# Half-height sums joined by the vector engine and added to the image in the transfer, in place of unit-matrix products

## The chip, the cores and the metric

The kernel runs on one core of a Trainium2 chip. Its engines are PE (TensorE, matrix products; PEld is its loading of weights), DVE (VectorE), ACT (ScalarE), POOL (GpSimd) and SP (SyncE, which here only issues transfers). They run side by side and wait for one another by semaphores. Inputs and output lie in HBM; SBUF is the core's memory and PSUM the store into which PE writes. The metric is the device time of one execution in microseconds; lower is better.

## What is computed

160 images of 128 channels x 32 x 32 in float32. Each is group-normalised (32 groups of 4 channels), convolved 3 x 3 with the weights of its set (image index modulo 5 chooses one of 5 sets), and added to itself. The weights are quantised in two steps from U, with step sizes s1 and s2 that come from U's range:

```python
def _L0_conv_ref(x, U):
    s1 = (jnp.max(U) - jnp.min(U)) / 3.0
    v1 = s1 * floor(U / s1)
    s2 = s1 / 5.0
    v2 = s2 * floor((U - v1) / s2)
    w = (v1 + v2).reshape(OUT_CH * N, IN_CH, 3, 3)
    xb = x.reshape(B // 5, 5 * 128, 32, 32)
    return conv(xb, w, padding=1, feature_group_count=5)   # back to x's shape

def _gn(v, G=32, eps=1e-5):
    ...   # (g - mean) / sqrt(var + eps) over 4 channels x 32 x 32
x = x + _L0_conv_ref(_gn(x), L0_conv_U)
```

## The kernel before

The channels lie on the 128 partitions, and an image is 1024 float32 numbers on each. The 160 images are taken set by set, 32 of each; four images make a chunk (2 MB, tile `xt`), and six chunks have room in SBUF. The kernel writes its own order: nothing is scheduled for it, and each engine takes its instructions in the order in which `run` emits them. One pass of the loop in `run` is called iteration i below.

The weights are kept as small whole numbers (5 k1 + k2) in float16, so that w = s2 times them; what makes them, `make_column`, is spread over 26 iterations of the set before, two DVE steps in each, and ends with transposes on PE (`pt`), copies by ACT (`wt`) and sums by POOL.

For image i the steps are:

- `measure`: mean and variance of each channel, 13 images ahead. For even images DVE does it (`image`: BATCH_NORM_STATS2 on two halves and one aggregate, lines 156 and 157); for odd images, and the first eight, ACT does it in two passes (`image_sum` line 163, `image_square` line 172) that write a `junk` tile, and POOL scales the sums (`minus`, `mv`). The square needs `minus` from POOL.
- Once per group of images (2, 2, 4, 4, 4, then 8): `means`, `deviations`, `variances`, `scales` average over 4 channels with two small products on PE, and POOL makes `rstd` and `shift` (lines 202 to 207). `rstd` carries a factor of 512.
- `normalise` and `high_part`: ACT makes z = rstd x + shift in float32 (line 428) and `hi`, z in float16 (line 436), three images ahead.
- `low_part` and `combinations`: DVE makes `lo` = z - hi in float16 (line 441), its differences between rows two apart `d`, and sums and differences of pairs of rows `st` (lines 455 to 458), two images ahead.
- `conv`: PE makes from `st` two half-height products in the bank `m` (6 matrix products), and then in the bank `eo` the direct part, 9 taps on `hi` and corrections from `d` (30 matrix products). There is room for one `m` and two `eo`.
- `leave` (line 528): ACT copies `m` to SBUF as float16, scaled by 2^-10. `add_pairs` (lines 531 to 541): DVE adds and subtracts the two halves into `pq` (lines 537, 538), and PE adds `pq` to `eo` by two products with `up`, a unit matrix times 0.5 x 2^10.
- `residual` (line 550): DVE makes xt = s2z eo + xt in place, one iteration later, where s2z = s2 / 512. After the fourth image of a chunk SP stores the chunk (line 557). The last four images are stored one by one.

Images 0 to 2 are convolved directly from `hi` and `lo` (`conv_direct`), before there are weights and sums for the rest. A second, general path (`general_path`) stands behind a branch that is taken only if the flag `far`, worked out from U's range, is set; it isn't with these inputs.

Of the kernel before, what the change touches and what calls it, by code (L numbers as in the profile page):

```python
# [8 lines left out]
F32 = mybir.dt.float32  # L9
# [12 lines left out]
NB = 4  # L22
SCALE = 512.0
DOWN = 2.0**-10

# [5 lines left out]
class Steps:  # L31


    def __init__(self, nc, pool):
        self.nc = nc
        self.pool = pool
        self.s1, self.s2, self.s2z = (self.col(tag) for tag in ("s1", "s2", "s2z"))
# [9 lines left out]
    def from_range(self, extg):  # L47
# [27 lines left out]
        yield from parts(self.parts2, self.s2)  # L75
        yield nc.vector.tensor_scalar_mul(self.s2z, self.s2, 1.0 / SCALE)
# [57 lines left out]
class Statistics:  # L134

    def __init__(self, nc, small, psum, gavg, mhalf, nb, scale, name):
        self.nc, self.small, self.psum, self.gavg, self.mhalf = nc, small, psum, gavg, mhalf
        self.nb, self.scale, self.name = nb, scale, name  # L140
        self.mv = self.tile("mv", [nb, 2])
        self.minus = {}
# [55 lines left out]
    def scales(self):  # L198
        nc = self.nc
        ve = self.tile("ve", [self.nb])  # L200
        nc.scalar.copy(ve, self.pg[:, 1, :])
        nc.gpsimd.tensor_scalar(ve, ve, EPS, self.scale**-2, ALU.add, ALU.mult)
        self.rstd = self.tile("rstd", [self.nb])
        nc.gpsimd.tensor_tensor(self.rstd, ve, self.mhalf[:, : self.nb], ALU.pow)  # L204

        self.shift = self.tile("shift", [self.nb])
        nc.gpsimd.tensor_tensor(self.shift, self.ngm, self.rstd, ALU.mult)  # L207
# [68 lines left out]
class Main:  # L276
# [13 lines left out]


    STAT_LEAD = 13
    LOAD_LEAD = 17
# [7 lines left out]
    def __init__(self, tc, ctx, keep, x, u, out):  # L301
# [25 lines left out]
        self.steps = Steps(nc, keep)  # L327
        self.chunks, self.z, self.hi, self.v, self.eo, self.m = {}, {}, {}, {}, {}, {}
        self.wts = {}

# [50 lines left out]
    def make_column(self, n, col):  # L381
# [14 lines left out]
        wt = self.wpool.tile([P, 6, P], MM, tag=f"wt{col}", name=f"wt{n}_{col}")  # L396
        nc.scalar.copy(wt[:, self.G, :], pt)  # L397
        nc.scalar.mul(wt[:, self.MINUS_G2, :], pt[:, 2, :], -1.0)
        outer = self.qpool.tile([P, P], MM, tag="outer", name=f"outer{n}_{col}")
# [3 lines left out]
        self.wts[n, col] = wt  # L403


    def measure(self, i, stages=(0, 1)):


        k = self.group_of[i]
        g = self.groups[k]  # L410
        if k not in self.stats:
            self.stats[k] = Statistics(
                self.nc, self.small, self.ps_stat, self.gavg, self.mhalf, len(g), SCALE, k
            )
        st, j, image = self.stats[k], i - g.start, self.image(i)
        if i % 2 == 0 and i >= self.EARLY:
            st.image(j, image)
            return
        for s in stages:
            junk = self.evac.tile([self.P, 1024], MM, tag="junk", name=f"junk{i}_{s}")  # L420
            (st.image_sum, st.image_square)[s](j, image, junk)
# [72 lines left out]
    def conv(self, i):  # L494
# [22 lines left out]
        for col in self.COLS:  # L517
            self.taps(i, (self.hi[i], 0), col, eo, False)
            for a, kind in enumerate((0, self.MINUS_G2)):
                for h in range(2):  # L520
                    rows = slice(h * 16 + a, h * 16 + 16, 2)
                    to = eo[:, h].rearrange("p (i a) w -> p i a w", a=2)[:, :, a, :]
                    product(to, kind, d[:, rows, :], col, False, False)

    def leave(self, i):

        m = self.evac.tile([self.P, 2, 512], MM, tag="mm", name=f"mm{i}")
        self.nc.scalar.mul(m, self.m.pop(i).rearrange("p a i w -> p a (i w)"), DOWN)  # L528
        self.m[i] = m

    def add_pairs(self, i):

        nc = self.nc
        m = self.m.pop(i).rearrange("p a (i w) -> p a i w", w=self.W)
        pq = self.evac.tile([self.P, 2, 512], MM, tag="pq", name=f"pq{i}")
        rows = pq.rearrange("p h (i a w) -> p (h i) a w", a=2, w=self.W)
        nc.vector.tensor_add(rows[:, :, 0], m[:, 0], m[:, 1])  # L537
        nc.vector.tensor_sub(rows[:, :, 1], m[:, 0], m[:, 1])  # L538
        for h in range(2):
            to = self.eo[i][:, h].rearrange("p r w -> p (r w)")  # L540
            nc.tensor.matmul(to, self.up, pq[:, h], start=False, stop=True)  # L541

    def residual(self, i):
        eo = self.eo.pop(i)
        del self.hi[i]
        n, b = self.place(i)
        xj = self.image(i)
        halves = [slice(0, 512), slice(512, 1024)] if i == self.imgs - 1 else [slice(0, 1024)]
        for h in halves:
            self.nc.vector.scalar_tensor_tensor(  # L550
                xj[:, h], eo.rearrange("p h r w -> p (h r w)")[:, h], self.steps.s2z,
                xj[:, h], ALU.mult, ALU.add,
            )
            if i >= self.imgs - NB:
                self.nc.sync.dma_start(self.ov[n, :, b, h], xj[:, h])
        if i < self.imgs - NB and i % NB == NB - 1:
            self.nc.sync.dma_start(
                self.ov[n, :, b - NB + 1 : b + 1, :], self.chunks[i // NB]
            )

    def run(self):
# [17 lines left out]
        nc.gpsimd.tensor_copy(self.ident, ident)  # L579

        self.up = self.const.tile([P, P], MM, tag="up", name="up")
        nc.gpsimd.tensor_scalar_mul(self.up, ident, 0.5 / DOWN)
        self.gavg = group_mean_matrix(nc, self.const)
# [72 lines left out]
        self.conv_direct(2, 0)  # L656
        run(self.make_column(0, 2))
        ready, middle, measured, loaded, later = [], [], self.EARLY, 3, None
        for i in range(self.imgs):
# [16 lines left out]
            for k in to_measure:  # L676
                if k % 2:
                    self.measure(k, (0,))
# [11 lines left out]
            if i >= self.FIRST:  # L690
                self.add_pairs(i)
            for st in middle:
# [67 lines left out]
```

## Time and profile before

| | |
|---|---|
| median of 3 runs | 1168.15 us (1167.84 to 1168.36) |
| profiled execution | 1166.93 us, its span 1165.2 us |
| mean granted PE clock | 0.993 |
| busy, of the span | PE 96%, DVE 83%, ACT 59%, POOL 20% |
| DMA engines' share, in the steady state | 0.42, at 155 GB/s |
| HBM read and written | 86.84 MB and 83.89 MB |

The span runs from the first to the last instruction. A busy share says only how long an engine worked, not whether anybody waited for it; the chain of work that ended last says which engine's work set the end. A row of the lists by line gives the line, engine, operation, output from inputs, shape and count, then busy microseconds and mean nanoseconds of one, then the engine's idle time before them and what ended it. The first 75 us are a start in which weights, first statistics and first images are made one after the other; the steady state runs from there to about 1158 us.

### The profile page before, as it was taken

The numbers are of one execution on the slowest core, as the hardware profiler recorded it, in microseconds if no ns is written. First come the engines' busy times: TensorE is split into PE (matmuls) and PEld (weight loads), VectorE is DVE, ScalarE is ACT, GpSimd is POOL, SyncE is SP. The second block draws the span as 40 slices with busy tenths as digits, with TensorE's granted clock in tenths as the row PEclk, the third lists the DMA queues.
The fourth block names the chain that finished last, engine by engine and source line by source line (L and its number), as shares of the span: only waits on it lengthen the run. The fifth ranks groups of instructions, "written<-read, shape, count | busy, mean of one in ns | idle before, by whom it ended". The sixth has DMA issues, their size and how long they took to land.

```text
span 1165.2 us, 15925 instructions
## 1 busy us (share of the span) xinstructions
PE 1116.1 (96%) x6215; PEld 610.4 (52%) x6215; DVE 962.5 (83%) x1626; ACT 690.4 (59%) x891; POOL 234.5 (20%) x450
## 2 busy tenths in 40 slices
PE   0679999999999999999999999999999999999997
PEld 0335555555555555555555555555555555555554
DVE  7878988887798989878888887798989877777662
ACT  4666666656666566655665666656656666655441
POOL 3413312121113121202122221123122202021100
PEclk9889999999999999999999999999999999999999
DMA  9204444444333333333344444444333333331222
GB/s 363 99 39 151 162 156 165 161 171 156 145 145 145 145 145 145 145 145 145 145 162 166 162 161 179 167 154 154 145 145 145 145 145 145 145 145 73 87 96 109
DMA packets 43427, 171.82 MB, mean 147 GB/s; under 512 B 1488, under 2 KB 1488, under 8 KB 43344
## 3 DMA queue, kind: packets, MB, share of 16 engines
q1 hardware_dynamic: 43344, 170.73, 39.1%
q8 instruction: 50, 0.82, 0.3%
q14 instruction: 33, 0.27, 0.1%
HBM read 86.84 MB, written 83.89 MB: 147 GB/s over the span
## 4 chain that ended last, share of the span: by engine, by line
PE 95%; DVE 3%; ACT 1%; DMA 1%; POOL 0%; issue 0%; SPq 0%; DVEq 0%
PE eo L475 52%; PE eo L502 18%; PE m L502 18%; PE eo L541 6%; PE m L475 1%; DMA u<-in_L_conv_U_dram 1%; DVE ext L361 0%; DVE ext L362 0%; DVE xt L550 0%; DVE lo L441 0%; PE pg L196 0%; PE pg L181 0%; POOL rstd L204 0%; PE pt L395 0%; ACT z L428 0%
## 5 line engine op out<-in xcount | busy, mean ns | idle before, releaser
L475 PE MATMUL eo<-hi,wt 128*128 128x512 f16 (+1 forms) x2862 | 685.5, 376 | 1.1 <-ACT wt L397 1.1
L475 PEld LDWEIGHTS <-wt 128*128 128x128 f16 x2934 | 288.0, 98 | 276.2 <-issue 5.0
L502 PEld LDWEIGHTS <-wt 128*128 128x128 f16 x2826 | 276.7, 99 | 219.0 <-issue 4.4
L528 ACT ACTIVATE mm<-m 128x1024 f16<-128x1024 f32 x157 | 160.5, 1022 | 366.8 <-PE m L502 355.1
L502 PE MATMUL eo<-d,wt 128*128 128x256 f16 (+1 forms) x1884 | 283.2, 273 | 0.0
L550 DVE SCALAR_TENSOR_TENSOR xt<-eo,s2z,xt 128x1024 f32<-128x1024 f32 (+1 forms) x160 | 203.5, 1273 | 47.9 <-PE eo L541 40.1
L502 PE MATMUL m<-st,wt 128*128 128x512 f16 x942 | 230.4, 381 | 3.2 <-DVE xt L550 3.2
L428 ACT ACTIVATE z<-xt,shift,rstd 128x1024 f32<-128x1024 f32 x160 | 198.0, 1237 | 31.1 <-POOL shift L207 31.1
L441 DVE TENSOR_TENSOR lo<-z,hi 128x1024 f16<-128x1024 f32 x160 | 194.1, 1214 | 5.3 <-ACT hi L436 5.2
L537 DVE TENSOR_TENSOR pq<-mm 128x512 f16<-128x512 f16 x157 | 66.4, 423 | 122.9 <-ACT mm L528 122.7
L436 ACT CAST hi<-z 128x1024 f16<-128x1024 f32 x160 | 166.1, 1038 | 0.2
L165 POOL TENSOR_SCALAR minus<-total 128x1 f32<-128x1 f32 x84 | 47.3, 563 | 340.9 <-ACT junk L163 340.7
L455 DVE TENSOR_TENSOR d<-lo 128x1024 f16<-128x1024 f16 x157 | 109.5, 697 | 5.4
L172 ACT ACTIVATE junk<-xt,minus 128x1024 f16<-128x1024 f32 x84 | 96.7, 1152 | 1.0 <-POOL minus L165 1.0
L156 DVE BATCH_NORM_STATS2 st<-xt 128x6 f32<-128x512 f32 x152 | 97.2, 681 | 0.0
L163 ACT ACTIVATE junk<-xt 128x1024 f16<-128x1024 f32 x84 | 88.0, 1048 | 11.8 <-DMA xt<-in_x_dram 11.7
L175 POOL TENSOR_SCALAR mv<-squares 128x1 f32<-128x1 f32 x84 | 45.7, 545 | 237.5 <-ACT junk L172 234.9
L541 PE MATMUL eo<-pq,up 128*128 128x512 f16 x314 | 93.5, 380 | 0.0
L538 DVE TENSOR_TENSOR pq<-mm 128x512 f16<-128x512 f16 x157 | 65.6, 418 | 0.0
L457 DVE TENSOR_TENSOR st<-lo 128x512 f16<-128x512 f16 x157 | 65.6, 418 | 0.0
L458 DVE TENSOR_TENSOR st<-lo 128x512 f16<-128x512 f16 x157 | 65.4, 416 | 0.0
L204 POOL TENSOR_TENSOR rstd<-ve,mhalf 128x8 f32<-128x8 f32 (+2 forms) x23 | 43.9, 1907 | 1.9
(87 smaller groups left out, 421.1 us busy)
## 6 DMA issues: line engine op xcount, KB each, us to landing
xt<-in_x_dram SPq DMA_DIRECT2D x39, 2048.0 KB, 13.0
out_dram<-xt SPq DMA_DIRECT2D x39, 2048.0 KB, 7.6
u<-in_L_conv_U_dram SPq DMA_DIRECT2D x4, 576.0 KB, 8.1
xt<-in_x_dram SPq DMA_DIRECT2D x4, 512.0 KB, 10.7
out_dram<-xt SPq DMA_DIRECT2D x3, 512.0 KB, 2.7
u<-in_L_conv_U_dram SPq DMA_DIRECT2D x2, 288.0 KB, 3.0
out_dram<-xt SPq DMA_DIRECT2D x2, 256.0 KB, 3.5
```

The lines of the kernel that those rows point to most:

```text
L156: self.nc.vector.bn_stats(st[:, h, :], image[:, h * half : (h + 1) * half])
L163: nc.scalar.activation(junk, image, ACTF.Copy, accum_out=total)
L172: nc.scalar.activation(junk, image, ACTF.Square, bias=self.minus[j], accum_out=squares)
L428: nc.scalar.activation(z, self.image(i), ACTF.Identity, bias=st.shift[:, j : j + 1], scale=st.rstd[:, j : j + 1],)
L436: self.nc.scalar.copy(hi.rearrange("p h w -> p (h w)"), self.z[i])
L441: self.nc.vector.tensor_sub(lo[:, 1 : self.H + 1, :].rearrange("p h w -> p (h w)"), self.z.pop(i), self.hi[i].rearrange("p h w -> p (h w)"),)
L455: nc.vector.tensor_sub(d, lo[:, 0:H, :], lo[:, 2 : H + 2, :])
L475: nc.tensor.matmul(target[:, h, r0 - h0 : r1 - h0, c0:c1], self.wts[n, col][:, k, :], tile[:, s0 : s0 + r1 - r0, c0 + dw : c1 + dw], start ...
L502: nc.tensor.matmul(target[:, :, c0:c1], self.wts[n, col][:, kind, :], source[:, :, c0 + dw : c1 + dw], start=start, stop=stop,)
L528: self.nc.scalar.mul(m, self.m.pop(i).rearrange("p a i w -> p a (i w)"), DOWN)
L541: nc.tensor.matmul(to, self.up, pq[:, h], start=False, stop=True)
L550: self.nc.vector.scalar_tensor_tensor(xj[:, h], eo.rearrange("p h r w -> p (h r w)")[:, h], self.steps.s2z, xj[:, h], ALU.mult, ALU.add,)
```

## The change

- `add_pairs` becomes `pairs`: DVE makes `pq` as before, but PE no longer adds it. `up` and its two products per image are gone, and `eo` is finished by its last correction from `d`.
- `residual` makes, one iteration later, sum = 0.5/32 pq + eo into a tile `sum` (three of them). `accumulate` then adds `sum` to the image in its chunk by a transfer from SBUF to SBUF with an addition, issued from POOL's queue at the end of iteration i + 1. The chunk's store moves to the end of iteration i + 2 and waits for its four additions.
- Images 0 to 2 and the last four (`by_hand`) are added by DVE itself; for the last four that is one more operation in `pairs`.
- The step size moves into the images: `rstd` is multiplied by 2^14 s2 (through `shrink` = (1/s2 / 2^14)^2, made by DVE in the start, and used by POOL's line 217 in each group's `scales`), and the weights by 2^-14. `s2z` is gone. `far` now also looks at the size of s2, and is worked out in `choose`, after the columns of the first set.
- DVE does the statistics of one image in four (8, 12, 16, ...) instead of one in two; ACT does the others. `junk` gets a pool of its own with one buffer.

```diff
-        yield nc.vector.tensor_scalar_mul(self.s2z, self.s2, 1.0 / SCALE)
-        big, far = col("big"), col("far")
-        yield nc.vector.tensor_reduce(big, extg, AX.X, ALU.max)
-        yield nc.vector.scalar_tensor_tensor(far, span, WIDEST, big, ALU.mult, ALU.is_lt)
-        yield nc.vector.tensor_copy(self.far, far)
+        r = self.parts2[0]
+        yield nc.vector.scalar_tensor_tensor(self.shrink, r, LIFT**-2, r, ALU.mult, ALU.mult)
+        self.span, self.big = span, col("big")
+        yield nc.vector.tensor_reduce(self.big, extg, AX.X, ALU.max)
...
-        nc.gpsimd.tensor_scalar(ve, ve, EPS, self.scale**-2, ALU.add, ALU.mult)
+        nc.gpsimd.tensor_scalar(ve, ve, EPS, self.shrink, ALU.add, ALU.mult)
...
+        self.sums = pool("sums", 3)
+        self.unread = pool("unread", 1)
...
-        nc.scalar.copy(wt[:, self.G, :], pt)
-        nc.scalar.mul(wt[:, self.MINUS_G2, :], pt[:, 2, :], -1.0)
+        nc.scalar.mul(wt[:, self.G, :], pt, 1.0 / LIFT)
+        nc.scalar.mul(wt[:, self.MINUS_G2, :], pt[:, 2, :], -1.0 / LIFT)
...
+    def by_vector(self, i):
+        return i % 4 == 0 and i >= self.EARLY
...
-        if i % 2 == 0 and i >= self.EARLY:
+        if self.by_vector(i):
...
-        for h in range(2):
-            to = self.eo[i][:, h].rearrange("p r w -> p (r w)")
-            nc.tensor.matmul(to, self.up, pq[:, h], start=False, stop=True)
+        self.m[i] = pq
+        if self.by_hand(i):
+            xj = self.image(i)
+            nc.vector.scalar_tensor_tensor(xj, pq, 0.5 / UP, xj, ALU.mult, ALU.add)
+
+    def by_hand(self, i):
+        return i < self.FIRST or i >= self.imgs - NB

     def residual(self, i):
...
+        if not self.by_hand(i):
+            self.sum[i] = self.sums.tile([self.P, 1024], F32, tag="sum", name=f"sum{i}")
+            nc.vector.scalar_tensor_tensor(
+                self.sum[i], self.m.pop(i), 0.5 / UP, eo, ALU.mult, ALU.add
+            )
+            return
...
-            self.nc.vector.scalar_tensor_tensor(
-                xj[:, h], eo.rearrange("p h r w -> p (h r w)")[:, h], self.steps.s2z,
-                xj[:, h], ALU.mult, ALU.add,
-            )
+            nc.vector.tensor_add(xj[:, h], eo[:, h], xj[:, h])
...
+    def accumulate(self, i):
+        if i in self.sum:
+            self.nc.gpsimd.dma_start(self.image(i), self.sum.pop(i), accum_op=ALU.add)
+
+    def store(self, i):
+        if 0 <= i < self.imgs - NB and i % NB == NB - 1:
...
+            self.accumulate(i - 1)
+            self.store(i - 2)
             while loaded * NB < min(self.imgs, i + self.LOAD_LEAD):
                 self.load(loaded)
```

On PE, where one image ends and the next begins, the order before is this (`up` is the unit matrix, `m` and `eo` the banks, `d` and `st` the combinations of `lo`):

```order
L502 MATMUL eo_4911<-d_4829,wt_2_4771 128x8x31
L541 LDWEIGHTS up
L541 MATMUL eo_4911<-pq_4962,up 128x512
L541 LDWEIGHTS up
L541 MATMUL eo_4911<-pq_4962,up 128x512
L502 LDWEIGHTS wt_1_3585
L502 MATMUL m_4973<-st_4890,wt_1_3585 128x512
```

And this is the same place now:

```order
L526 LDWEIGHTS wt_2_4875
L526 MATMUL eo_5288<-d_5196,wt_2_4875 128x8x31
L526 LDWEIGHTS wt_2_4875
L526 MATMUL eo_5288<-d_5196,wt_2_4875 128x8x31
L526 LDWEIGHTS wt_1_3659
L526 MATMUL m_5365<-st_5259,wt_1_3659 128x512
```

The next image's first half product follows the last correction directly; nothing on PE reads `pq`.

On SP, in the middle of the program, stores and loads of chunks alternated like this before (the first number in a name is the chunk's):

```order
L557 DMA out_0_dram<-xt13_3039 128x4x1024
L346 DMA xt18_4424<-in_x_dram 128x4x1024
L557 DMA out_0_dram<-xt14_3302 128x4x1024
L346 DMA xt19_4704<-in_x_dram 128x4x1024
L557 DMA out_0_dram<-xt15_3600 128x4x1024
```

And now like this:

```order
L599 DMA out_0_dram<-xt12_2815 128x4x1024
L366 DMA xt18_4517<-in_x_dram 128x4x1024
L599 DMA out_0_dram<-xt13_3102 128x4x1024
L366 DMA xt19_4803<-in_x_dram 128x4x1024
L599 DMA out_0_dram<-xt14_3371 128x4x1024
```

The store of a chunk now stands one load later: the load of chunk 18 followed the store of chunk 13, and now follows that of chunk 12, whose room it takes.

On POOL, the statistics of consecutive images read now as follows (there was no transfer on this queue before):

```order
L594 DMA xt_1969<-sum_3229 128x1024
L594 DMA xt_1969<-sum_3291 128x1024
L180 TENSOR_SCALAR minus_3346<-total_3344 128x1
L181 TENSOR_SCALAR mv_3013<-total_3344 128x1
L190 TENSOR_SCALAR mv_3013<-squares_3365 128x1
L594 DMA xt_1969<-sum_3359 128x1024
L180 TENSOR_SCALAR minus_3416<-total_3414 128x1
```

An addition stands between one image's last statistic and the next one's first.

More of the change, by code (lines that the diff above doesn't have):

```diff
@@ L22 @@
 NB = 4
-SCALE = 512.0
-DOWN = 2.0**-10
+LIFT = 2.0**14
+LEAST, MOST = 2.0**-10, 0.06
+UP = 32.0
 WIDEST = 40.0
@@ L36, in __init__ @@
         self.pool = pool
-        self.s1, self.s2, self.s2z = (self.col(tag) for tag in ("s1", "s2", "s2z"))
+        self.s1, self.s2, self.shrink = (self.col(tag) for tag in ("s1", "s2", "shrink"))
         self.parts1, self.parts2 = (
@@ L75, in from_range, with choose @@
         yield from parts(self.parts2, self.s2)
-        yield nc.vector.tensor_scalar_mul(self.s2z, self.s2, 1.0 / SCALE)
-        big, far = col("big"), col("far")
-        yield nc.vector.tensor_reduce(big, extg, AX.X, ALU.max)
-        yield nc.vector.scalar_tensor_tensor(far, span, WIDEST, big, ALU.mult, ALU.is_lt)
-        yield nc.vector.tensor_copy(self.far, far)
+        r = self.parts2[0]
+        yield nc.vector.scalar_tensor_tensor(
+            self.shrink, r, LIFT**-2, r, ALU.mult, ALU.mult
+        )
+        self.span, self.big = span, col("big")
+        yield nc.vector.tensor_reduce(self.big, extg, AX.X, ALU.max)
+    def choose(self):
+        nc, far = self.nc, self.col("far")
+        nc.vector.scalar_tensor_tensor(
+            far, self.span, WIDEST, self.big, ALU.mult, ALU.is_lt
+        )
+        for limit, op in ((MOST, ALU.is_gt), (LEAST, ALU.is_lt)):
+            nc.vector.scalar_tensor_tensor(far, self.s2, limit, far, op, ALU.max)
+        nc.vector.tensor_copy(self.far, far)
     def floor_div(self, k, v, n, t, parts):
@@ L134, with __init__ @@
 class Statistics:
-    def __init__(self, nc, small, psum, gavg, mhalf, nb, scale, name):
+    def __init__(self, nc, small, psum, gavg, mhalf, nb, shrink, name):
         self.nc, self.small, self.psum, self.gavg, self.mhalf = nc, small, psum, gavg, mhalf
-        self.nb, self.scale, self.name = nb, scale, name
+        self.nb, self.shrink, self.name = nb, shrink, name
         self.mv = self.tile("mv", [nb, 2])
@@ L328, in __init__ @@
         self.chunks, self.z, self.hi, self.v, self.eo, self.m = {}, {}, {}, {}, {}, {}
+        self.sum = {}
         self.wts = {}
@@ L412, in measure @@
             self.stats[k] = Statistics(
-                self.nc, self.small, self.ps_stat, self.gavg, self.mhalf, len(g), SCALE, k
+                self.nc, self.small, self.ps_stat, self.gavg, self.mhalf, len(g),
+                self.steps.shrink, k,
             )
         st, j, image = self.stats[k], i - g.start, self.image(i)
-        if i % 2 == 0 and i >= self.EARLY:
+        if self.by_vector(i):
             st.image(j, image)
@@ L419, in measure @@
         for s in stages:
-            junk = self.evac.tile([self.P, 1024], MM, tag="junk", name=f"junk{i}_{s}")
+            junk = self.unread.tile([self.P, 1024], MM, tag="junk", name=f"junk{i}_{s}")
             (st.image_sum, st.image_square)[s](j, image, junk)
@@ L676, in run @@
             for k in to_measure:
-                if k % 2:
+                if not self.by_vector(k):
                     self.measure(k, (0,))
@@ L690, in run @@
             if i >= self.FIRST:
-                self.add_pairs(i)
+                self.pairs(i)
             for st in middle:
```

22 lines of the change are left out of this document (12 added, 10 removed).

## The prediction

> **What bounds the kernel now.** I read the page's busy line and its chain first, then the order of time on PE in the steady state, then the groups by line, then the other engines' load in one window.
>
> ```profile
> PE 1116.1 (96%) x6215; PEld 610.4 (52%) x6215; DVE 962.5 (83%) x1626; ACT 690.4 (59%) x891; POOL 234.5 (20%) x450
> PE 95%; DVE 3%; ACT 1%; DMA 1%; POOL 0%; issue 0%; SPq 0%; DVEq 0%
> L541 PE MATMUL eo<-pq,up 128*128 128x512 f16 x314 | 93.5, 380 | 0.0
> L528 ACT ACTIVATE mm<-m 128x1024 f16<-128x1024 f32 x157 | 160.5, 1022 | 366.8 <-PE m L502 355.1
> ```
>
> PE is busy for 96% of the span and makes 95% of the chain: from the first product on, the other engines only matter if they make PE wait. L528 waits 355.1 us for PE: ACT is ahead of it. The products to be removed are the 314 of L541. Their 380 ns each overlaps the next product, so the price is read from start to start (columns: start, duration, engine, line):
>
> ```profile
> 502.99 0.60 PE L541 MATMUL eo<-pq,up 128*128 128x512 f16 x2
> 503.42 1.46 PE L502 MATMUL m<-st,wt 128*128 128x512 f16 x6
> 509.84 0.60 PE L541 MATMUL eo<-pq,up 128*128 128x512 f16 x2
> 510.27 1.46 PE L502 MATMUL m<-st,wt 128*128 128x512 f16 x6
> ```
>
> A pair holds PE for 503.42 - 502.99 = 0.43 us, and an image takes 509.84 - 502.99 = 6.85 us.
>
> **Term 1, the products.** 157 images x 0.43 us = 67.5 us less on PE, all of it on the chain. An image then takes 6.42 us. Whether this is gained depends on what must now fit into 6.42 us.
>
> **DVE.** The columns are the window and its length, then busy time of PE, PEld, DVE, ACT and POOL, the granted clock, the DMA engines' share and GB/s.
>
> ```profile
> 300.00:600.00 300.00, 300.00 (x1689) 165.05 (x1687) 260.91 (x443) 185.24 (x237) 63.65 (x114) 1.00 0.42 155
> L550 DVE SCALAR_TENSOR_TENSOR xt<-eo,s2z,xt 128x1024 f32<-128x1024 f32 (+1 forms) x160 | 203.5, 1273 | 47.9 <-PE eo L541 40.1
> L156 DVE BATCH_NORM_STATS2 st<-xt 128x6 f32<-128x512 f32 x152 | 97.2, 681 | 0.0
> L157 DVE BATCH_NORM_AGGREGATE mv<-st 128x2 f32<-128x12 f32 x76 | 15.9, 209 | 4.0
> ```
>
> 300 us hold 300 / 6.85 = 43.8 images, so DVE works 260.91 / 43.8 = 5.96 us an image. The residual becomes an operation of the same size with one operand in PSUM and one in SBUF, as L550 has; I take its 1.27 us unchanged. The bounds are L550's own 1.27 us from below and, from above, 0.2 us more: such a slip would still fit. One image in four no longer has the statistics on DVE: (2 x 0.681 + 0.209) / 4 = 0.39 us less an image. That leaves 5.57 of 6.42 us, 87%, the share it has now. DVE's cover is thin but no thinner than before, and PE no longer waits for `pq` at all: the pair sums now feed the vector engine alone. What is queued behind DVE's wait for `eo` is as before. The four images added by hand at the end cost an extra 1.27 us each on DVE, where the last weights are long done; I count nothing, the cover being PE's 6.42 us an image.
>
> **ACT.** These rows are one image's ACT work with a statistics pass in it.
>
> ```profile
> 649.20 1.24 ACT L428 ACTIVATE z<-xt,shift,rstd 128x1024 f32<-128x1024 f32 x1
> 650.34 1.05 ACT L163 ACTIVATE junk<-xt 128x1024 f16<-128x1024 f32 x1
> ...
> 651.37 1.02 ACT L528 ACTIVATE mm<-m 128x1024 f16<-128x1024 f32 x1
> 652.28 1.05 ACT L436 CAST hi<-z 128x1024 f16<-128x1024 f32 x1
> 653.21 1.16 ACT L172 ACTIVATE junk<-xt,minus 128x1024 f16<-128x1024 f32 x1
> ...
> 654.36 1.24 ACT L428 ACTIVATE z<-xt,shift,rstd 128x1024 f32<-128x1024 f32 x1
> ```
>
> From z to z are 654.36 - 649.20 = 5.16 us. This is now wanted for three images of four instead of two. The pass is 651.37 - 650.34 = 1.03 plus 654.36 - 653.21 = 1.15, so the mean rises from 185.24 / 43.8 = 4.23 to 4.23 + 2.18 / 4 = 4.78 us of 6.42. Even the full image leaves 1.26 us. In iteration 8 the statistics of images 17, 18 and 19 come at once: two more passes make ACT up to 4.4 us late; the `m` bank is wanted back only when the next image begins, 6.42 less the 1.3 us of its products less 1.02 us of L528, about 4 us after ACT could first read it. I count nothing, with 1 us as the upper bound.
>
> **The transfers.** 153 images are added by a transfer from SBUF to SBUF issued on POOL's queue.
>
> ```profile
> q1 hardware_dynamic: 43344, 170.73, 39.1%
> xt<-in_x_dram SPq DMA_DIRECT2D x39, 2048.0 KB, 13.0
> out_dram<-xt SPq DMA_DIRECT2D x39, 2048.0 KB, 7.6
> xt<-in_x_dram SPq DMA_DIRECT2D x4, 512.0 KB, 10.7
> out_dram<-xt SPq DMA_DIRECT2D x3, 512.0 KB, 2.7
> ```
>
> The share of 0.42 is 0.42 x 6.85 = 2.88 us of all 16 engines an image, for 512 KB in and 512 KB out: 1.44 us for each. No row shows an adding transfer. From below it is a plain copy, 1.44 us; from above, unknown, call it f x 1.44. At f = 2, which I take because it moves one operand more than a copy, 5.76 of 6.42 us are used, 0.90, and nothing waits. DMA becomes the bound at f = (6.42 - 2.88) / 1.44 = 2.5 and eats the whole gain at (6.85 - 2.88) / 1.44 = 2.8.
> The Trainium skill's page "Collectives: The Full Stack", section "The bandwidth ceiling: the fold count and why AG ≠ RS ≠ AR", says that an addition in a DMA engine is slow only because it reads two sources, 1.93 times the cost of a copy there; by it f is about 2 and the sum stays. No run here shows it yet.
>
> Latency: an addition leaves at the latest one iteration after its sum and the three `sum` tiles give it two more, 12.8 us, against a landing of 2.7 us (a 512 KB store) to 10.7 us (a queued 512 KB load). SP's queue: the store now waits for the four additions, and the load behind it goes into the tile that is being stored, where before it went into one stored a chunk earlier. From the start of iteration 4c+5 the longest rows give 10.7 + 13.0 + 13.0 = 36.7 us, 5.7 images, so the load lands by 4c+10.7; its first reader is the statistic of image 4c+24 in iteration 4c+11. From below it is 2.7 + 7.6 + 7.6 = 17.9 us. Zero either way.
>
> **POOL.** It gets 153 issues, each behind a wait for DVE's sum; queued behind it are the next image's `minus` (for which ACT's square waits) and, eight images apart, `ve`, `rstd`, `shift`. In the rows above a square ends at 654.4 and the next one starts at 653.21 + 6.42 = 659.6; issue and `minus` must fit between, so an issue of up to 5 us costs nothing. No row shows one; the nearest, other POOL operations of 0.21 to 1.75 us (below), fit.
>
> **Term 2, the start.** `ve` of the first group now needs `shrink`, which DVE makes after the parts of s2, about where it made `s2z`.
>
> ```profile
> 26.04 0.36 POOL L202 TENSOR_SCALAR ve<-ve 128x2 f32<-128x2 f32 x1
> 27.48 0.14 DVE L76 TENSOR_SCALAR s2z<-s 128x1 f32<-128x1 f32 x1
> 37.65 1.23 DVE L441 TENSOR_TENSOR lo<-z,hi 128x1024 f16<-128x1024 f32 x1
> 68.37 1.28 DVE L156 BATCH_NORM_STATS2 st<-xt 128x6 f32<-128x512 f32 x2
> 69.68 0.21 DVE L157 BATCH_NORM_AGGREGATE mv<-st 128x2 f32<-128x12 f32 x1
> 69.81 1.17 DVE L441 TENSOR_TENSOR lo<-z,hi 128x1024 f16<-128x1024 f32 x1
> 73.62 2.72 PE m L502 x6
> ```
>
> `ve` moves from 26.04 to about 27.6, +1.6 us, and the first images behind it (the `lo` at 37.65 waits for them). Against it, image 10 leaves DVE, 69.81 - 68.37 = 1.4 us on the way to the first half product at 73.62; though ACT now does that pass, 2.18 us, and could give back 0.8 of it. Three tiny operations leave the chain (`far` comes back later, while DVE idles) and `shrink` joins it: 0.3 us less. Sum about 0, bounds -1.7 and +2.4.
>
> **Sum.** The profiled execution took 1166.93 us (span 1165.2 and 1.7 around it); 1166.9 - 67.5 = 1099.4. The median of the runs is 1.2 us above it, so 1100.6.
>
> **Rivals.**
> *A, the additions fill the DMA engines (slower).* For it: 0.42 is already used and an adding transfer reads more than it copies. Against: f must pass 2.8. At f = 3 an image takes 2.88 + 4.32 = 7.2 us, 157 x 0.35 = +55: 1223 us.
> *B, POOL's issues hold up DVE (slower).* These are POOL beside DVE:
>
> ```profile
> 307.28 1.75 POOL L204 TENSOR_TENSOR rstd<-ve,mhalf 128x8 f32<-128x8 f32 x1
> 307.42 1.22 DVE L441 TENSOR_TENSOR lo<-z,hi 128x1024 f16<-128x1024 f32 x1
> 316.30 1.17 POOL L166 TENSOR_SCALAR mv<-total 128x1 f32<-128x1 f32 x1
> 316.19 1.22 DVE L441 TENSOR_TENSOR lo<-z,hi 128x1024 f16<-128x1024 f32 x1
> 18.72 0.21 POOL L175 TENSOR_SCALAR mv<-squares 128x1 f32<-128x1 f32 x1 [0.92 <-ACT junk L172]
> ```
>
> A one-element POOL operation takes 0.21 us alone and 1.17 us under a DVE subtraction, ending with it: POOL is held by DVE. The other way is not seen: `lo` began 0.14 us into `rstd` and still took 1.22 us. If an issue did hold DVE for the longest of these, 1.75 us, DVE would need 5.57 + 1.75 = 7.32 us in the 128 images of the sets with weights in the making: +0.47 x 128 = +60, less 0.43 x 29 = 12: 1216 us. It decides from an issue of 6.85 - 5.57 = 1.28 us.
> The Trainium skill's page "SBUF — State Buffer", section "Who interferes with whom", states the lock for both sides: whoever starts first has the shared ports for the whole instruction. By it rival B would be likely; the row at 307.42 disagrees with it, that at 316.30 agrees.
> *C, part of the gain is lost at group and column starts.* z waits there for POOL's chain, and ACT's copies of weights wait for PE:
>
> ```profile
> ACT z L428 <- POOL shift L207: 31.1, 17, 3.8
> ACT wt L397 <- PE pt L395: 45.3, 15, 3.8
> ```
>
> If PE lost 0.6 us at each of these 32 places, 19 us would come back: 1120 us. Against it: L528's wait of 355.1 us, which is ACT's lead.
>
> **Chances.** Forecast 0.72, holding 1095 to 1106 (1100.6 with -1.7 to +2.4 of the start, 1 of ACT and the spread of runs, and small slips). C 0.10 (1106 to 1130). A 0.12: of it 0.02 lies between f of 2.5 and 2.8, still faster, and 0.10 is slower; B 0.04 slower; 0.02 that gains and losses cancel. A measurement of this kernel tells 0.2% (2.3 us) from no change. Faster 0.84, within 0.2% 0.02, slower 0.14. The range 1095 to 1127 leaves out A and B, a little of C and the low tail.
>
> **What would show it.** Right: PE's chain share still above 90%, image to image 6.42 us, no L541-like group, DVE near 87% and ACT near 75% in the steady window, DMA share near 0.9, and no row of PE waiting for ACT or DVE after 80 us. Term 2: POOL's first `ve` at about 27.6. Wrong: a DMA share of 1.0 with SP or DVE waiting for `sum` tiles (A); `lo`, `d` or `pq` longer than 1.22, 0.7 and 0.42 us beside POOL's issues (B); PE idle before `m` on ACT (C).

## The result and the profile after

The changed kernel takes 1100.56 us, the median of 4 runs (1100.23 to 1101.58), against 1168.07 us (1167.84 to 1168.36) for the kernel before: ratio 0.9423, 95% interval 0.9407 to 0.944. The forecast was 1100.6. The profiled execution took 1101.58 us, its span 1099.8 us.

The page of the changed kernel: busy time by engine, the new DMA queue (packets, MB, share of 16 engines' span), the chain by engine, the two largest new groups, and two kinds of DMA issue (count, KB each, us from issue to landing).

```profile
PE 1051.8 (96%) x5901; PEld 577.6 (53%) x5901; DVE 903.9 (82%) x1518; ACT 772.9 (70%) x1043; POOL 389.4 (35%) x716
...
q0 software_dynamic: 22032, 80.23, 38.9%
...
PE 94%; DVE 3%; DMA 1%; POOL 0%; ACT 0%; issue 0%; SPq 0%; DVEq 0%
...
L581 DVE SCALAR_TENSOR_TENSOR sum<-pq,eo 128x1024 f32<-128x1024 f16 x153 | 185.9, 1215 | 16.0 <-PE eo L526 15.8
...
L594 POOL DMA_DIRECT2D xt<-sum x153 | 136.6, 894 | 85.4 <-DVE sum L581 69.5
...
xt<-in_x_dram SPq DMA_DIRECT2D x39, 2048.0 KB, 13.5
...
xt<-sum POOLq DMA_DIRECT2D x153, 512.0 KB, 8.0
```

PE has 314 instructions fewer (5901 for 6215) and still makes 94% of the chain. The work that it lost rides along in DVE's residual, which is now the sum (L581, no longer than L550 was); adding to the image went to a new queue, q0, issued by POOL (L594), which takes 38.9% of what the 16 DMA engines have. The loads beside it land in 13.5 us where they took 13.0.

The steady window, with the columns of the one shown before, and then, from the order of time on PE, the starts of two images:

```profile
300.00:600.00 300.00, 300.00 (x1708) 165.89 (x1706) 259.16 (x440) 223.01 (x299) 114.44 (x195) 1.00 0.88 244
```

```profile
504.34 1.46 PE L526 MATMUL m<-st,wt 128*128 128x512 f16 x6
...
510.76 1.46 PE L526 MATMUL m<-st,wt 128*128 128x512 f16 x6
```

PE is busy for all of the 300 us at full clock. An image takes 510.76 - 504.34 = 6.42 us instead of 6.85. DVE stands at 259.16 / 300 = 86%, ACT at 74%, the DMA engines at 0.88 instead of 0.42.

The start, on PE, after and before: the first half product of image 3, and that of image 4.

```profile
74.07 2.72 PE L526 MATMUL m<-st,wt 128*128 128x512 f16 x6 [1.94 <-DVE xt L588]
...
83.55 1.46 PE L526 MATMUL m<-st,wt 128*128 128x512 f16 x6
```

```profile
73.62 2.72 PE L502 MATMUL m<-st,wt 128*128 128x512 f16 x6 [3.18 <-DVE xt L550]
...
82.28 1.46 PE L502 MATMUL m<-st,wt 128*128 128x512 f16 x6
```

Image 3 starts 0.45 us later than before. Its own length, to the start of image 4, is 9.48 us after and 8.66 us before, where 6.56 and 6.99 would be normal (6.42 and 6.85, with 0.14 for a small product in between). So image 3 loses 2.92 us to a slow clock, against 1.67 before: 1.25 more. Together the start costs +1.7 us in these two executions.

### The profile page after: what moved, and what is told of

Its sections match the earlier page's. It is cut to its first block, busy times and chain, and to the rows that moved or that the text cites. A ratio compares the mean times of both kernels' runs of the same rounds, so it can differ in the third digit from the quotient of the medians.

```text
span 1099.8 us, 16007 instructions
## 1 busy us (share of the span) xinstructions
PE 1051.8 (96%) x5901; PEld 577.6 (53%) x5901; DVE 903.9 (82%) x1518; ACT 772.9 (70%) x1043; POOL 389.4 (35%) x716
## 3 DMA queue, kind: packets, MB, share of 16 engines
q0 software_dynamic: 22032, 80.23, 38.9%
## 4 chain that ended last, share of the span: by engine, by line
PE 94%; DVE 3%; DMA 1%; POOL 0%; ACT 0%; issue 0%; SPq 0%; DVEq 0%
PE eo L499 55%; PE eo L526 19%; PE m L526 19%; PE m L499 1%; DMA u<-in_L_conv_U_dram 1%; DVE ext L381 0%; DVE ext L382 0%; DVE xt L588 0%; DVE lo L465 0%; PE pg L211 0%; PE pt L415 0%; ACT z L452 0%; PE pg L196 0%; ACT hi L460 0%; POOL rstd L219 0%
## 5 line engine op out<-in xcount | busy, mean ns | idle before, releaser
L465 DVE TENSOR_TENSOR lo<-z,hi 128x1024 f16<-128x1024 f32 x160 | 194.6, 1217 | 8.6 <-ACT hi L460 8.4
L581 DVE SCALAR_TENSOR_TENSOR sum<-pq,eo 128x1024 f32<-128x1024 f16 x153 | 185.9, 1215 | 16.0 <-PE eo L526 15.8
L190 POOL TENSOR_SCALAR mv<-squares 128x1 f32<-128x1 f32 x122 | 67.4, 553 | 313.8 <-ACT junk L187 311.3
L594 POOL DMA_DIRECT2D xt<-sum x153 | 136.6, 894 | 85.4 <-DVE sum L581 69.5
L187 ACT ACTIVATE junk<-xt,minus 128x1024 f16<-128x1024 f32 x122 | 140.5, 1152 | 2.5 <-POOL minus L180 1.5
L178 ACT ACTIVATE junk<-xt 128x1024 f16<-128x1024 f32 x122 | 127.7, 1047 | 11.3 <-DMA xt<-in_x_dram 11.1
L180 POOL TENSOR_SCALAR minus<-total 128x1 f32<-128x1 f32 x122 | 42.0, 345 | 107.1 <-ACT junk L178 106.3
L171 DVE BATCH_NORM_STATS2 st<-xt 128x6 f32<-128x512 f32 x76 | 48.6, 680 | 0.0
L181 POOL TENSOR_SCALAR mv<-total 128x1 f32<-128x1 f32 x122 | 44.4, 364 | 0.1
## 6 DMA issues: line engine op xcount, KB each, us to landing
xt<-in_x_dram SPq DMA_DIRECT2D x39, 2048.0 KB, 13.5
```

The lines of the kernel that those rows point to most:

```text
L178: nc.scalar.activation(junk, image, ACTF.Copy, accum_out=total)
L187: nc.scalar.activation(junk, image, ACTF.Square, bias=self.minus[j], accum_out=squares)
L190: nc.gpsimd.tensor_scalar_mul(self.mv[:, j, 1:2], squares, 1.0 / image.shape[1])
L465: self.nc.vector.tensor_sub(lo[:, 1 : self.H + 1, :].rearrange("p h w -> p (h w)"), self.z.pop(i), self.hi[i].rearrange("p h w -> p (h w)"),)
L581: nc.vector.scalar_tensor_tensor(self.sum[i], self.m.pop(i), 0.5 / UP, eo, ALU.mult, ALU.add)
L594: self.nc.gpsimd.dma_start(self.image(i), self.sum.pop(i), accum_op=ALU.add)
```

## The experiments

The theory was that the whole change is worth PE's 67.5 us because the rest stays hidden. Three questions follow from it: is it the products alone, which of the other parts does it need, and how much room is left in what hides the transfer. The fourth is the start, where the forecast's sum was off. "On the same chip" below is the kernel before, in that set of runs.

### Is it the products? Two products put back

`zero_products` adds to each image two products with a matrix of zeros, where those with `up` were, and leaves the rest of the change.

```diff
...
+        for h in range(2):
+            to = eo[:, h].rearrange("p r w -> p (r w)")
+            src = self.hi[i][:, h * 16 : h * 16 + 16, :].rearrange("p r w -> p (r w)")
+            nc.tensor.matmul(to, self.zero, src, start=False, stop=True)
```

> The changed kernel with two extra products per image into eo (512 columns, weights all zero, moving operand hi, at the place where the unit-matrix products stood); nothing else changes. Theory 1 (the whole gain is PE time, 157 x 0.43 us): 1100.6 + 67.5 = 1168, within 3 us. Rival (the gain came mainly from PE no longer waiting for pq, that is from the vector engine leaving PE's path): these products wait for nothing, so the time would stay clearly below 1168, at 1140 or less.

Measured: 1168.53 us (1167.16 to 1169.58, 10 runs), on the same chip 1166.2; ratio 1.0018 (1.0008 to 1.0027). Its group on the page:

```profile
L552 PE MATMUL eo<-hi,zero 128*128 128x512 f16 x314 | 93.5, 380 | 0.0
```

It is the row of the removed L541 again, to the nanosecond, and the whole gain is gone. What is left over, 0.9 to 3.1 us above the kernel before, fits the start: in this run's profile the half product of image 4 begins at 83.33 us, 1.05 us later than before.

### Which other parts does the gain need?

`add_by_dve` lets DVE add every image itself, with no transfer; `stats_half` gives DVE the statistics of every second image again; `before_stats_quarter` is the kernel before with statistics on DVE for one image in four.

```diff
# add_by_dve, in by_hand
-        return i < self.FIRST or i >= self.imgs - NB
+        return True
# stats_half, in by_vector
-        return i % 4 == 0 and i >= self.EARLY
+        return i % 2 == 0 and i >= self.EARLY
# before_stats_quarter, in the kernel before
-        if i % 2 == 0 and i >= self.EARLY:
+        if i % 4 == 0 and i >= self.EARLY:
...
-                if k % 2:
+                if k % 4 or k < self.EARLY:
```

> The changed kernel with every image added by hand: DVE adds pq to the image in pairs and eo to it in residual; no adding transfers. Theory 1 with DVE as the next bound: DVE's 259.16 us per 300 us window is 5.55 us an image of 6.42, plus one more operation of 1.2 us = 6.75 us: DVE becomes the bound at about 1100.6 + 157 x 0.33 = 1152, and since the weights' steps are uneven (none in the last set) 1140 to 1165. Rival (DVE's waits give way, so that the extra operation hides): 1101 to 1105. Second rival (the two-operation image costs as much as the products saved): 1168.

> The changed kernel with DVE taking the statistics of every second image again (8, 10, 12, ...). Theory 1: DVE needs 5.55 + 0.39 = 5.94 us of 6.42 on average, 93%, and the time stays within 0.5% of 1100.6 (1100 to 1106). Rival (a quarter was needed as cover: with steps of weights and statistics in one iteration DVE needs 7.3 us and falls behind for good): 1120 or more.

> The kernel before with DVE taking the statistics of one image in four, the only part of the change made. Theory 1: PE sets the time, so 1168 within 2 us; at most 1.5 us less from image 10 leaving DVE in the start. Rival (the fewer vector statistics are a gain of their own): 1160 or less.

| | us (range, runs) | ratio (interval) |
|---|---|---|
| add_by_dve | 1160.99 (1159.56 to 1161.41, 4) | 0.9947 (0.9931 to 0.9964) |
| stats_half | 1101.46 (1099.35 to 1101.73, 4) | 0.9435 (0.9419 to 0.9451) |
| before_stats_quarter | 1165.7 (1163.74 to 1167.14, 10) | 0.9992 (0.9982 to 1.0001) |

The steady window of `add_by_dve`, and the chain on its page:

```profile
300.00:600.00 300.00, 284.17 (x1579) 154.71 (x1577) 290.07 (x446) 206.40 (x279) 76.62 (x146) 0.98 0.39 152
```

```profile
DVE 59%; PE 34%; issue 3%; ACT 2%; POOL 2%; DMA 1%; SPq 0%; DVEq 0%
```

DVE is at 290.07 of 300 us and makes 59% of the chain: it has become the bound. PE idles for 16 us of the window. Without the transfer 60 of the 67.5 us are lost, 0.39 us an image: it is the transfer that lets the products go.

The same window of `stats_half`:

```profile
300.00:600.00 300.00, 300.00 (x1707) 165.96 (x1706) 274.87 (x476) 198.07 (x252) 103.97 (x160) 1.00 0.89 245
```

DVE stands at 92% and PE still never waits. Moving the statistics gave nothing, with the transfer or, in `before_stats_quarter`, without it.

### What does the addition cost the DMA engines, and how near is the bound?

`plain_copy` sends the same transfer without the addition; it leaves out adding the sum to x, so the image is overwritten by the sum. `dma_half_more` and `dma_whole_more` send, behind each addition, a plain transfer of 256 KB or 512 KB of the sum to scratch memory in HBM.

```diff
# plain_copy
-            self.nc.gpsimd.dma_start(self.image(i), self.sum.pop(i), accum_op=ALU.add)
+            self.nc.gpsimd.dma_start(self.image(i), self.sum.pop(i))
# dma_half_more (:512), dma_whole_more (:1024)
+            sum = self.sum.pop(i)
+            self.nc.gpsimd.dma_start(self.image(i), sum, accum_op=ALU.add)
+            self.nc.gpsimd.dma_start(self.more[i % 8, :, :512], sum[:, :512])
```

> The changed kernel with the transfer of sum copying over the image instead of adding to it (this leaves out the addition of x to the convolution), everything else and all waits as before. The adding transfers took 38.9% of 16 engines for 153 x 512 KB, 2.80 us each by share, against 1.40 us for a plain load or store. If reading two operands is what doubles it: about 1.4 us, 20% of the engines, landing in 4 to 6 us instead of 8.0, SP's waits shorter, and the time unchanged at 1100.6 within 2 us, because transfers are hidden. Rival (the SBUF-to-SBUF path or the software queue is slow in itself): still near 38%. Second rival (DMA load slows the kernel a little already): 1095 or less.

> The changed kernel with one more plain transfer per image on POOL's queue, 256 KB of sum to a scratch in HBM that nobody reads. DMA work per image by share: 5.65 + 0.70 = 6.35 us of 6.42, 0.99. Theory: just at the edge, 1100 to 1112. Rival (queues and latency make it break before the share reaches 1): 1120 or more. Rival (POOL's extra issue of 0.9 us counts): the same sign, but then POOL, not the sum tiles, is waited for.

> The same with 512 KB more per image: 5.65 + 1.40 = 7.05 us of 6.42. Theory: DMA becomes the bound and DVE waits for sum tiles; 1100.6 + 153 x 0.63 = 1197, 1180 to 1215. Rival (the share counts latency, not occupancy, and there is room left): 1101 to 1110.

| on the same chip 1167.31 | us (range, runs) | ratio (interval) |
|---|---|---|
| plain_copy | 1100.69 (1098.66 to 1101.65, 4) | 0.9433 (0.9417 to 0.9448) |
| dma_half_more | 1101.87 (1099.33 to 1102.69, 4) | 0.9433 (0.9417 to 0.9448) |
| dma_whole_more | 1116.0 (1112.73 to 1118.44, 4) | 0.9552 (0.9534 to 0.957) |

The queue and the transfer of `plain_copy`, on its page:

```profile
q0 software_dynamic: 22032, 80.23, 18.1%
...
xt<-sum POOLq DMA_DIRECT2D x153, 512.0 KB, 4.7
```

The same packets and bytes take 18.1% of a span of 1096.9 us, 1.30 us of the 16 engines an image; with the addition 38.9% of 1099.8, 2.80 us. The addition makes the transfer 2.15 times as dear, and the time is the same: it is hidden.

The steady window of `dma_half_more`:

```profile
300.00:600.00 300.00, 300.00 (x1705) 165.81 (x1704) 258.12 (x438) 223.05 (x300) 140.81 (x242) 1.00 0.98 284
```

The same of `dma_whole_more`; then its two queues, the chain and the stores on its page; then three of its waits (total us, count, longest us):

```profile
300.00:600.00 300.00, 292.70 (x1650) 160.63 (x1649) 252.43 (x425) 216.53 (x290) 135.77 (x234) 0.99 1.02 313
```

```profile
q0 software_dynamic: 44064, 160.45, 54.9%
q1 hardware_dynamic: 43344, 170.73, 40.5%
...
PE 67%; DMA 19%; DVE 10%; issue 2%; POOL 1%; ACT 1%; SPq 0%; DVEq 0%; POOLq 0%
...
out_dram<-xt SPq DMA_DIRECT2D x39, 2048.0 KB, 21.4
```

```profile
DVE st L171 <- DMA xt<-in_x_dram: 69.0, 22, 6.6
ACT junk L178 <- DMA xt<-in_x_dram: 59.5, 20, 11.5
...
DVE sum L581 <- DMA more<-sum: 11.4, 10, 2.0
```

The kernel with half more moves 256 KB more an image at a share of 0.98 and loses nothing that can be told. With a whole one more the transfers are the bound: the chain has 19% of DMA, the first statistics of a chunk wait for its load (69.0 and 59.5 us), the load stands on SP behind the store, and the store's landing grew to 21.4 us. It is the loads above all that come late; the `sum` tiles, which were expected to, make DVE wait for only 11.4 us.

The price was far less than expected: 1116 us, not 1197. The share explains the miss in two parts. First, the transfers took less of it than was added up: 0.549 x 1116.6 / 153 = 4.0 us an image for the addition and the extra transfer, and about 2.8 us for load and store (40.5% of the span, without the loads of U), 6.8 us in all where 7.05 was expected. Second, these 6.8 us pass in the 6.42 + (1116.0 - 1100.6) / 157 = 6.52 us that an image takes on the average. So the share counts about 4% more than there is, and it goes to 1.02 in the window: packets must overlap in it.

### How thin is the cover of the `sum` tiles?

```diff
# two_sums
-        self.sums = pool("sums", 3)
+        self.sums = pool("sums", 2)
```

> The changed kernel with two sum tiles instead of three. An addition is issued about 5 us into the iteration after its sum's (measured at 504.3 and 510.4 us) and lands 8.0 us later in the median; with three tiles the tile is wanted back 14.5 us after the issue, with two 8 us after it. Theory: the cover is gone, DVE waits for landings in part of the images; 1103 to 1140. Rival (landings are quick enough, or DVE's slack of 0.9 us an image takes it): 1100.6 within 2 us.

Measured: 1104.37 us (1103.21 to 1106.06, 4 runs), ratio 0.9458 (0.9442 to 0.9474), on the same chip as the three above. Among DVE's waits stands a row that the changed kernel hasn't:

```profile
DVE sum L581 <- DMA xt<-sum: 70.7, 47, 4.0
```

The columns are again total us, count and longest us: 47 times DVE waits for the transfer to give a tile back, 1.5 us on the average and 4.0 at the longest. DVE's spare time swallows most of the 70.7 us; on PE, behind the start, only the wait of `pt` (the transposes of weights) for DVE grew, from 4.8 us in one wait to 7.3 in two. The 3 to 4 us by which the median lies above the changed kernel, which was measured on other chips, are about 0.3%, hardly more than can be told. The forecast of 1103 to 1140 holds at its lower end.

### The start

Image 3's half product waits for DVE's residual of image 2 (1.94 us, `xt L588`), which stands on DVE behind the `lo`, `d` and `st` of image 4. `residual_first` emits that residual ahead of them. `residual_first_filled` does the same and puts 12 products that nobody reads into PE's wait.

```diff
+            if i == self.FIRST - 1:                      # filled only, after conv(i)
+                fill = self.ps_tr.tile([P, 512], F32, tag="pt", name="fill")
+                src = self.hi[i][:, 0:16, :].rearrange("p r w -> p (r w)")
+                for _ in range(12):
+                    nc.tensor.matmul(fill, self.ident, src, start=True, stop=True)
...
+            if i == self.FIRST - 1:                      # both, ahead of low_part(i + 2)
+                self.residual(i)
...
-            if i < self.FIRST:
+            if i < self.FIRST - 1:
                 self.residual(i)
```

> The changed kernel, unchanged, for comparison on this chip: 1100 to 1101.

> The changed kernel with the residual of image 2 emitted ahead of the low part and combinations of image 4. The first half product of the steady state waits for that residual (PE's m waits 1.9 us at 74.07); DVE then does it at about 70.3 instead of 72.8. PE still needs the total of image 11 (a mean product at 71.75). Theory: m starts at about 72.2, 1.9 us less in all, 0.2% (1098.7). Rival (the granted clock, which is low from 74 to 80 us after PE's wait, is not lowered after a shorter wait): 3 us more, 1095.5. Second rival (the combinations of image 4 come late and PE waits at image 4): no gain.

> The same, with 12 products into a bank nobody reads (unit matrix on hi, about 2.6 us) in PE's wait after the third direct image. Theory (the slow products from 74 to 80 us come from the idle time, and filled idle time keeps the clock): the first six m products take 1.3 instead of 2.7 us and the next six 1.3 instead of 2.7; 3 us less than residual_first, 1095.5. Rival (a wait of about 3 us lowers nothing, or 0.7 us of idle time left do so): as residual_first.

| on the same chip 1166.52 | us (range, runs) | ratio (interval) |
|---|---|---|
| after_again, unchanged | 1101.38 (1098.97 to 1102.02, 5) | 0.9437 (0.9424 to 0.9449) |
| residual_first | 1097.28 (1095.99 to 1097.64, 5) | 0.9405 (0.9392 to 0.9418) |
| residual_first_filled | 1095.42 (1094.3 to 1096.46, 5) | 0.939 (0.9377 to 0.9402) |

The order of time on PE from the last direct products (`m<-lo`) to image 4 in `after_again`, and its window from 70 to 80 us (the third number from the end is the granted clock); then the same of `residual_first` and of `residual_first_filled`:

```profile
67.94 1.44 PE L499 MATMUL m<-lo,wt 128*128 128x496 f16 x6
72.09 0.38 PE L196 MATMUL pg<-mv,gavg 128*128 128x4 f32 x2 [2.71 <-POOL mv L181]
...
74.41 2.72 PE L526 MATMUL m<-st,wt 128*128 128x512 f16 x6 [1.94 <-DVE xt L588]
...
83.72 0.59 PE L526 MATMUL m<-st,wt 128*128 128x512 f16 x2
```

```profile
70.00:80.00 10.00, 5.97 (x17) 2.52 (x18) 8.59 (x14) 7.05 (x10) 1.76 (x6) 0.66 0.00 0
```

```profile
66.85 1.44 PE L499 MATMUL m<-lo,wt 128*128 128x496 f16 x6
70.34 0.39 PE L196 MATMUL pg<-mv,gavg 128*128 128x4 f32 x2 [2.05 <-POOL mv L181]
70.76 2.13 PE L526 MATMUL m<-st,wt 128*128 128x512 f16 x6
...
79.01 1.46 PE L526 MATMUL m<-st,wt 128*128 128x512 f16 x6
```

```profile
70.00:80.00 10.00, 9.62 (x45) 4.91 (x46) 9.79 (x17) 7.13 (x10) 2.23 (x8) 0.83 0.00 0
```

```profile
67.38 1.44 PE L499 MATMUL m<-lo,wt 128*128 128x496 f16 x6
68.65 2.75 PE L715 MATMUL fill<-hi,ident 128*128 128x512 f16 x12
...
71.38 1.46 PE L526 MATMUL m<-st,wt 128*128 128x512 f16 x6
...
77.94 1.46 PE L526 MATMUL m<-st,wt 128*128 128x512 f16 x6
```

```profile
70.00:80.00 10.00, 10.00 (x57) 5.42 (x56) 9.79 (x17) 8.21 (x13) 2.34 (x8) 1.00 0.00 0
```

In `after_again` PE is idle for 2.71 + 1.94 us with one small product between, and the mean clock of the ten microseconds is 0.66; from `m` to `m` are 9.31 us. With the residual first, 2.05 us of idle time are left, and `m` to `m` takes 8.25 us. With the wait filled, it is 6.56 us, and the clock stays at 1.00 in this window. Against the normal 6.56 us the slow clock costs 2.75, 1.69 and 0 us.

The three executions stood apart before this place already, so the times are best counted from the start of their last direct products. From there `m` starts after 6.47, 3.91 and 4.00 us: the filling itself delays it by 0.09 us. The second `m` comes after 15.78, 12.16 and 10.56 us, which is 3.62 and 5.22 us earlier than in `after_again`. The medians differ by 4.10 and 5.96 us; the 0.5 and 0.7 us between are within the spread of the runs. The forecast for `residual_first`, 1098.7 or 1095.5, was missed in between: 2.6 us of waiting went, not 1.9, and a part of the slow clock with it. `residual_first_filled` came out at the 1095.5 that was forecast, but lies 1.86 us below `residual_first` instead of 3, and the runs of the two overlap a little. It has the lowest median of all, 6.0 us below `after_again` and 71 below the kernel before.

The Trainium skill's page "TensorE: Matmul & The Clock Gate", section "Part 1: The HAM clock gate", says that PE falls to half rate after an idle window of about 3.4 us and returns after one as long of work. The rows agree in kind: 4.65 us of idle time cost 2.75 us, filled time costs none. But 2.05 us of idle time and a small product were already enough to lose 1.69 us. By the granted clock the half rate lasted from 71.4 to 74.8 us in `residual_first`, which is as long as the page's window, and from 73.2 to 80.0 us in `after_again`, twice as long.

## Why the prediction was right, step by step

- **Term 1, 67.5 us of products: right.** The row of the pair put back is the same, and with it the gain is gone; the steady image takes the 6.42 us that start-to-start reading gave.
- **DVE: right, with a little more room.** The sum takes 1.215 us where L550's 1.27 was assumed; 86% of the window against 87. That the statistics had to move was neither needed nor claimed: at 92% DVE is still no bound (`stats_half`). At 97% it is (`add_by_dve`).
- **ACT and POOL: right.** ACT is at 223.01 / 300 = 74%, as worked out. An issue takes 0.89 us, far from the 5 us between squares.
- **Transfers: right.** The share is 0.88 where 0.90 was worked out. In the prediction's unit of 1.44 us the addition has f = 2.80 / 1.44 = 1.94, where 2 was taken; against a plain copy on the same path (1.30 us, `plain_copy`) it is 2.15. The bounds of 2.5 and 2.8 took a share of 1 for the limit; with the 1.04 of `dma_whole_more` they become (6.42 x 1.04 - 2.88) / 1.44 = 2.6 and (6.85 x 1.04 - 2.88) / 1.44 = 2.9, an estimate, so rival A was a little further off than it said. The Trainium skill's page "Collectives: The Full Stack", section "The bandwidth ceiling: the fold count and why AG ≠ RS ≠ AR", has 1.93 for its case; the 2.15 measured here is near it.
- **Latency: right.** The landing is 8.0 us, between the 2.7 and 10.7 named; three tiles are enough, two are not quite. SP's chain of store and load, which was worked out and put at zero, costs nothing here; in `dma_whole_more` it gives way first.
- **Rival B fell by the row it named.** POOL and DVE in the changed kernel:

```profile
509.21 1.22 DVE L465 TENSOR_TENSOR lo<-z,hi 128x1024 f16<-128x1024 f32 x1
509.35 1.15 POOL L190 TENSOR_SCALAR mv<-squares 128x1 f32<-128x1 f32 x1 [2.58 <-ACT junk L187]
510.44 0.90 POOL L594 DMA_DIRECT2D xt<-sum  x1
510.46 0.69 DVE L479 TENSOR_TENSOR d<-lo 128x1024 f16<-128x1024 f16 x1
```

  The `d` beside the issue takes 0.69 us, as ever; over the whole run the means of `lo`, `d` and the two `pq` are 1217, 695, 423 and 417 ns, and were 1214, 697, 423 and 418. POOL's small scaling is held for 1.15 us by `lo`, as before; the issue holds nobody, and at 0.90 us it would not have reached the 1.28 us from which B decided.
- **Rival C fell:** PE is busy for 300.00 of 300 us, at group and column starts too.
- **Term 2, the start: the one term that was off.** It was put at 0 with bounds of -1.7 and +2.4, and is +1.7 in the two executions compared above. The steps that the prediction named came as it said. This is the first `ve` in the changed kernel, then in its second profiled execution, `after_again`:

```profile
26.89 0.29 POOL L217 TENSOR_SCALAR ve<-ve,shrink 128x2 f32<-128x2 f32 x1 [1.37 <-DVE big L86]
```

```profile
27.60 0.29 POOL L217 TENSOR_SCALAR ve<-ve,shrink 128x2 f32<-128x2 f32 x1 [1.34 <-DVE big L86]
```

  In `after_again` it starts at the 27.6 us that were forecast. In the first execution it is 0.7 us earlier, but there everything is: PE's first product (`rows`), which waits for DVE's extremes of U, starts at 17.94 us, against 18.67 in `after_again` and 18.87 in the kernel before. Image 10's 1.4 us came back as well: from the residual of image 1 to that of image 2 DVE takes 72.81 - 69.11 = 3.70 us, where it took 72.29 - 67.17 = 5.12.

  What the sum had no term for is PE's clock, and it counts twice. The first place is the direct products of image 1: the transposes `pt` ahead of them start 0.95 us later than before (46.77 against 45.82), the mean product behind them 1.96 us later (54.94 against 52.98), so 1.0 us more is lost in between. The granted clock is at half from 45.9 to 52.7 us there, and was from 42.9 to 49.7. The second place is image 3, with 1.25 us more. These windows show where its slow stretch begins and ends, in the kernel before and then in the changed one (the third number from the end is the granted clock):

```profile
70.00:72.00 2.00, 0.41 (x2) 0.38 (x3) 1.97 (x4) 0.00 (x0) 0.00 (x0) 0.55 0.00 0
76.00:78.00 2.00, 2.00 (x9) 0.85 (x8) 0.67 (x3) 1.62 (x2) 0.00 (x0) 0.74 0.00 0
```

```profile
72.00:74.00 2.00, 0.13 (x2) 0.07 (x2) 2.00 (x5) 1.93 (x3) 0.21 (x1) 0.80 0.00 0
80.00:82.00 2.00, 2.00 (x13) 1.15 (x12) 1.97 (x4) 1.02 (x2) 0.89 (x2) 0.99 0.00 0
```

  A clock that changes between 1 and 0.5 gives these means if it is at half from 70.2 to 77.0 us before and from 73.2 to 80.0 us now. Image 3 begins at 73.62 and 74.07 us, so 3.4 and 5.9 us of the stretch lie on its products. Half of that is lost, 1.7 and 3.0 us, near the 1.67 and 2.92 measured. PE is not idle for longer ahead of it than it was (2.74 + 1.94 us, before 3.00 + 3.18); the slow stretch only lies later, on work instead of on waiting. Where it lies varies between executions: in `plain_copy`, which starts with the same instructions, image 3 loses 2.22 us. So the +1.7 is of these two executions, and no run shows how much of the clock's part is the change's own. That idle time is what brings the slow clock at this place, `residual_first_filled` shows.

With the measured terms the spans agree: 1165.2 - 67.5 + 1.7 = 1099.4, measured 1099.8. The median came out at 1100.56 and the forecast at 1100.6 with two small errors that cancel: +1.7 for the start was missing, and the 1.2 us by which the profiled run before lay under its median were added, where the profiled run after lies 1.0 us above its own. That the figure agrees to 0.1 us is luck; that it agrees to 2 us is Term 1. On the chip of `after_again` the same change is worth 1166.52 - 1101.38 = 65.1 us, near the 65.8 that Term 1 and the start give.

## What to carry to other kernels

Where one engine makes 95% of the chain, read the price of what leaves it from start to start, and spend the effort on what must fit into the shorter period: here an engine's load per image, the DMA engines' operands per image, and the latency against the number of buffers. An addition in a transfer is a way to take work off both PE and DVE as long as the DMA engines have room for somewhat over two plain transfers. In a start, look at the engine's clock behind each wait: once the order of the work is right, products that nobody reads can save what the slow clock still costs.

## What the runs showed of the hardware

- A transfer from SBUF to SBUF with an addition takes 2.80 us of the 16 DMA engines for 512 KB, against 1.30 us without (38.9% and 18.1% of the span, same packets), and lands in 8.0 us against 4.7.
- The DMA engines' share is no exact measure of what is left: at 0.98 (`dma_half_more`) the time was the same, and it reached 1.02 (`dma_whole_more`). The bound showed as waits for loads (69.0 us) and stores that land in 21.4 us.
- Issuing such a transfer takes POOL 0.89 us, and DVE's operations beside it keep their length.
- PE's granted clock was at half for stretches of 3.4 us (`residual_first`, 71.4 to 74.8) and 6.8 us (before, 70.2 to 77.0; after, 73.2 to 80.0). The loss was half of what lay on products: 1.69, 1.67 and 2.92 us.
- Twelve products in 2.75 us of PE's wait kept the clock at 1.00 and saved the 1.69 us that the slow clock had cost; they delayed the product that waited by 0.09 us.
